# Edge attention on one core: the order of VectorE's steps in a round, and 186 column tiles in place of 169

## The chip, the cores and the metric

The kernel runs on one core of one Trainium2 chip. The metric is the device time of one execution in microseconds (us), the median of several runs. The core's engines work from queues of their own and wait for each other by semaphores: TensorE (PE, with its weight loads as PEld), VectorE (DVE), ScalarE (ACT), GpSimd (POOL) and SyncE (SP, which only issues DMAs here).

## The reference

A graph attention layer with a residual and a layer norm: 6250 nodes, 206250 edges sorted by destination, 128 features in 8 heads of 16.

```python
Qh = (h @ WQ).reshape(N, H, D); Kh = (h @ WK).reshape(N, H, D); Vh = (h @ WV).reshape(N, H, D)
Eh = (edge_attr @ WE).reshape(-1, H, D)
score = jnp.einsum('ehd,ehd,ehd->eh', Kh[src], Qh[dst], Eh) * inv_sqrt_d
score = jnp.exp(jnp.clip(score, -5.0, 5.0))
wV = segment_sum(Vh[src] * score[:, :, None], dst);  Z = segment_sum(score, dst)
return _layernorm(x + (wV / (Z[:, :, None] + 1e-06)).reshape(N, H * D))
```

## The kernel before

**Tiles and batches.** The edges lie in 1612 tiles of 128 edges, one edge in each partition. Four tiles make a batch; the last eight tiles make smaller ones, so that there are 406 batches. The main loop (L616) makes one round for each batch `b`, and the instructions of each engine run in the order in which the rounds write them: from batch 12 on the order is the one written by hand (L618).

**Where K and V of an edge come from.** Each edge needs the K and V rows of its source node. A table `kv` of both lies in HBM (L262). `gather` (L412) fetches the rows of one tile with one indirect DMA that GpSimd issues (L421), into the tile `kvrows` of the batch, two rounds ahead (`GLEAD`). From batch 18 on, a gather may start only when the batch `lag(b)` before it has had its Q rows expanded (L424, L350): the lag falls from 12 batches to 3 at batch 162, one batch in 16 rounds.

**Column tiles.** For 169 tiles there is no gather. The transposed node features lie in SBUF as `xz`: two f32 for each node, its feature and a zero. `columns` (L375) copies the column of each edge's source node into the tile `xcol`, and TensorE multiplies it with the K and V weights (L403); ScalarE then copies the product into `kvrows` (L410). ScalarE copies one column with one instruction (L394). VectorE copies two with one: it takes 8 bytes that begin with one node's feature and 8 bytes that end with the other's, and ors them (L390). The place of a column is known only on the chip: its offset is loaded into registers, one instruction for each group of columns (`addresses`, L363; the load is L369), and the loads of the next group stand in the queue ahead of the copies of this one (L381 to L394). A column tile is cut into 16 groups of 8: ScalarE copies ten, VectorE six (`COLV`). The first column tile is batch 26's, and then there is one in every 2.2 batches (`COLP`). `columns(b, v, most)` writes as many groups of engine `v` as are due at round `b`, at most `most`.

**A round on VectorE**, in the order of the queue: K times Q of batch b-1, from `kvrows` and the expanded Q in PSUM (L500); in even rounds the one-hots of two batches (`stage_0`, L461); one step of small work (`fill`, L608: a step of the bf16 split of Q rows, L297 to L300, or of a layer norm, L773 to L793); the product with the edge features (`kqe`, L503); in odd rounds the transposed one-hots of two batches (`stage_0t`, L477); a group of columns; a `fill`; the sum over each head (L506); a group of columns; the messages of batch b-2 (L548); what columns are still due; a `fill`; the clip of batch b-1 (L509); a `fill`. K times Q writes `kq`, which `kqe` reads; `kqe` writes what the head sum reads; the clip reads the head sum.

**The other engines in a round.** TensorE expands Q of batch b (L489, one PSUM bank, free when K times Q has read it), projects the edge features (L494, one bank, free when `kqe` has read it), now and then adds up windows of finished nodes (`finish`, L529), adds the messages of batch b-2 (L570), and projects a column tile (L403) and Q rows (L293). ScalarE copies finished windows (L541), raises the clipped scores of batch b-1 to their exponentials (`weigh`, L515 into the single PSUM tile `exp_p` and L517 into the message tile), copies the column tile's K and V (L410), copies its groups of columns (L394), and copies finished sums (L580). The layer norm of two blocks of nodes begins with L773, one round after the second of their `finish`.

Of the kernel before, what the change touches and what calls it, by code (L numbers as in the profile page):

```python
# [8 lines left out]
F32 = mybir.dt.float32  # L9
I32 = mybir.dt.int32  # L10
BF16 = mybir.dt.bfloat16
U8 = mybir.dt.uint8
# [4 lines left out]
P = 128  # L17
# [5 lines left out]
HW = 64  # L23
HALF = 16
DRIFT = 24
LEFT, RIGHT = 43, 128
XC = LEFT + N + RIGHT
MW = D + H
CH = 8
# [21 lines left out]
QLOOK = 3  # L51
QREG = 16
COL0 = 26
COLP = (11, 5)
COLN = 8
COLV = 6
COLL = 8
RING = 4096
SUMS = 8
XT_AT = RING + P  # L60
# [3 lines left out]
def cut_batches():  # L64
    out, t = [], 0
    while t < NT:
        k = B
        if t >= NT - TAIL:
            k = 2 if NT - t > 3 else 1
        out.append(range(t, t + k))  # L70
        t += k
    return out


def column_tiles():

    batches = cut_batches()
    at = (COL0 + k * COLP[0] // COLP[1] for k in range(len(batches)))
    return [batches[b][-1] for b in at if b < len(batches) and batches[b][-1] < NT - TAIL - 4 * B]
# [23 lines left out]
def edge_attention(ctx: ExitStack, tc: tile.TileContext, x, xT, srcT, srcC, dstT, dstB, dst0, bnd, lo, eaT,  # L103
                   wq, wkv, we, out, kv, qtab, qs, relD):
    nc = tc.nc
# [33 lines left out]
    with ExitStack() as fast:  # L139
# [102 lines left out]
        wp = fast.enter_context(tc.tile_pool(name="work", bufs=3))  # L242
# [61 lines left out]
        def build_q(until, now):  # L304

            while qwork or (now and len(built) < until):
                if not qwork:
                    qwork.append(q_rows(len(built)))
                if next(qwork[0], None) is None:
                    qwork.pop()  # L310
                if not now:
                    break
# [23 lines left out]
        def load_chunk(c):  # L336
            if c in chunks or c * CH >= NT:
                return
            n = min(CH, NT - c * CH) * P
            tl = ep.tile([P, CH * P], F32, name="ea")  # L340
            nc.sync.dma_start(tl[:, :n], eaT[:, c * CH * P:c * CH * P + n])
            chunks[c] = tl
# [11 lines left out]
        col_tiles, xz_bytes = {}, xz.rearrange("p n z -> p (n z)").bitcast(U8)  # L354
# [1 line left out]

        copied, projected = [0, 0], []

        runs = P // COLN
        kinds = [range(runs - COLV), range(runs - COLV, runs)]  # L360
        ahead = [None, None]

        def addresses(v):  # L363

            k, j = divmod(copied[v], len(kinds[v]))
            if k >= len(col_batches):
                return None
            j = kinds[v][j] * COLN
            return nc.values_load_multi_w_load_instructions(  # L369
                col_at[k % col_half:k % col_half + 1, k // col_half, j:j + COLN],  # L370
                engines=((mybir.EngineType.Activation, mybir.EngineType.DVE)[v],),
                min_val=XT_AT + 8 * LEFT - 4, max_val=XT_AT + 8 * (LEFT + N - 1),
                skip_runtime_bounds_check_because="edges name nodes")[1]

        def columns(b, v, most=runs):  # L375

            mine = kinds[v]
            due = int((b - COL0 + COLL) * len(mine) * COLP[1] / COLP[0] + 1e-6)
            while most and copied[v] < min(due, len(col_batches) * len(mine)):
                k, j = divmod(copied[v], len(mine))  # L380
                at = ahead[v] or addresses(v)  # L381
                copied[v] += 1
                ahead[v] = addresses(v)
                most -= 1
                if k not in col_tiles:
                    col_tiles[k] = wp.tile([P, P], F32, name="xcol", bufs=5)
                to, j = col_tiles[k].bitcast(U8), mine[j] * COLN
                if v:
                    for c in range(0, COLN, 2):
                        nc.vector.tensor_tensor(to[:, 4 * (j + c):4 * (j + c) + 8], xz_bytes[:, ds(at[c] - XT_AT, 8)],  # L390
                                                xz_bytes[:, ds(at[c + 1] - XT_AT, 8)], op=ALU.bitwise_or)
                else:
                    for c in range(COLN):
                        nc.scalar.copy(to[:, 4 * (j + c):4 * (j + c) + 4], xz_bytes[:, ds(at[c] - XT_AT, 4)])  # L394

        def project_columns(b):

# [8 lines left out]
        def place_columns():  # L406

            while projected:
                g, pk = projected.pop()
                nc.scalar.copy(g[:, B - 1, :], pk)  # L410
# [135 lines left out]
        def messages(b):  # L546
            n, g, m = st8[b]
            nc.vector.tensor_tensor(  # L548
                m[:, :n, :D].rearrange("p b (h d) -> p b h d", h=H),
                g[:, :n, D:].rearrange("p b (h d) -> p b h d", h=H),  # L550
                exp_p[:, :n, :, None].to_broadcast([P, n, H, DH]), op=ALU.mult)
# [47 lines left out]
        build_q(q_built(QLOOK + 2), True)  # L599
        nc.sync.dma_start(col_at, srcC.rearrange("(h p) e -> p h e", h=2))  # L600
        nc.vector.tensor_scalar(col_at, col_at, 8, XT_AT + 8 * LEFT, op0=ALU.mult, op1=ALU.add)
        odd = col_at[:, :, (runs - COLV) * COLN:].rearrange("k h (c z) -> k h c z", z=2)[:, :, :, 1]
        nc.vector.tensor_scalar(odd, odd, 4, None, op0=ALU.subtract)
        load_rel(0)
        for j in range(QLOOK):
# [2 lines left out]
        def fill():  # L608

            if qwork:  # L610
                build_q(0, False)
            elif norms and next(norms[0], None) is None:
                norms.pop(0)

        held = []
        for b in range(nbat + 3):  # L616
            if b >= XB and not manual:
                manual.append(fast.enter_context(tc.manual_schedule()))  # L618
            held += [(b + SLAG, store) for store in stores]
            stores.clear()  # L620
            if held and (held[0][0] <= b or b >= nbat):
                held.pop(0)[1]()
            if b < nbat:
                load_chunk(batches[b][0] // CH + EB - 3)
                load_rel(batches[b][0] // RC + 1)
                load_q(batches[b][0] // WT + QLOOK)
                g = gathered.pop(b)
                if b == min(XB, nbat - 1):
                    late_loads()
                if b == min(XB + 8, nbat - 1):  # L630
                    relative(C0, NT)
                if b == 14:
                    from_window(1)
                if b == 0:
                    stage_0t(0)
                stage_a(b, g)
                if b + GLEAD < nbat and b + GLEAD not in gathered:
                    gathered[b + GLEAD] = gather(b + GLEAD)
            norms.extend(pending)
            pending.clear()  # L640
            for _ in range(len(ready) if b >= nbat - 2 else 1):
                if ready:
                    finish(ready.pop(0))
            steps = stage_b(b - 1) if 0 <= b - 1 < nbat else iter(())
            next(steps, None)
            if b < nbat:
                stage_0(b)
            fill()
            next(steps, None)
            if b + 1 < nbat:  # L650
                stage_0t(b + 1)
            if b < nbat:
                columns(b, 1, 1)
            fill()
            next(steps, None)
            if b < nbat:
                columns(b, 1, 1)
            if 0 <= b - 2 < nbat:
                messages(b - 2)
            if b < nbat:  # L660
                columns(b, 1)
            fill()
            next(steps, None)
            fill()
            if 0 <= b - 1 < nbat:
                weigh(b - 1)
            place_columns()
            if b < nbat:
                columns(b, 0)
            if 0 <= b - 2 < nbat:  # L670
                stage_c(b - 2)
            if b < nbat:
                project_columns(b + GLEAD)
                build_q(q_built(min(NJ - 1, batches[b][0] // WT + QLOOK + 2)), True)
                if not qwork and len(built) < q_built(
                        min(NJ - 1, batches[min(nbat - 1, b + 3)][0] // WT + QLOOK + 2)):
                    qwork.append(q_rows(len(built)))
                    next(qwork[0])
            if b == min(60, nbat):
                count_inside()  # L680
            if b == min(80, nbat + 1):
                inside = nc.values_load(cnt_i[0:1, 0:1], min_val=0, max_val=2 * EPAD,
                                        skip_runtime_bounds_check_because="two counts of EPAD edges")
# [159 lines left out]
```

## Time and profile before

| what | value |
|---|---|
| time, median of 3 runs | 1865.27 us (1862.6 to 1865.44) |
| time of the profiled execution | 1863.48 us |
| its span, first to last instruction | 1861.6 us |
| mean granted TensorE clock | 0.927 |
| DVE, ACT, POOL, PE busy | 92%, 85%, 74%, 71% of the span |
| gathers issued by POOL | 1395 from `kv`, 48 from `x` at the start |
| pairs of columns on DVE, columns on ACT | 4056, 13520 |

The page of the profile gives the busy time of each engine and the costliest groups of instructions: count, busy time (overlaps counted once), mean duration of one, and the idle time of the engine just before them with what ended it. The duration of an instruction on DVE or ACT overlaps with the start of the next, so that the step from one start to the next is shorter than the duration. Loads into registers are instructions of an engine's sequencer (DVEq, ACTq) and are not counted as busy. A releaser called "issue" means that the engine waited for nothing that the profile shows other than its own sequencer.

### The profile page before, as it was taken

The numbers are of one execution on the slowest core, as the hardware profiler recorded it, in microseconds if no ns is written. First come the engines' busy times: TensorE is split into PE (matmuls) and PEld (weight loads), VectorE is DVE, ScalarE is ACT, GpSimd is POOL, SyncE is SP. The second block draws the span as 40 slices with busy tenths as digits, with TensorE's granted clock in tenths as the row PEclk, the third lists the DMA queues.
The fourth block names the chain that finished last, engine by engine and source line by source line (L and its number), as shares of the span: only waits on it lengthen the run. The fifth ranks groups of instructions, "written<-read, shape, count | busy, mean of one in ns | idle before, by whom it ended". The sixth has DMA issues, their size and how long they took to land.

```text
span 1861.6 us, 49514 instructions
## 1 busy us (share of the span) xinstructions
PE 1324.9 (71%) x9388; PEld 1156.1 (62%) x9388; DVE 1710.0 (92%) x7312; ACT 1576.9 (85%) x14716; POOL 1379.2 (74%) x1450
## 2 busy tenths in 40 slices
PE   5877777677677767777767776776767676777775
PEld 4766666566566666666656665665656665666665
DVE  6579999999999999999999999999999999999986
ACT  3327999899999999999999999999989998999950
POOL 7777777767777777677777777777777777777774
PEclk8888998899999999899998899899999999999997
DMA  9767677667766776677677667767766676677652
GB/s 303 228 214 217 184 217 206 197 187 207 212 199 183 212 214 184 209 214 208 183 225 210 190 188 225 206 184 211 224 202 185 202 223 190 196 200 233 205 173 68
DMA packets 170093, 377.79 MB, mean 203 GB/s; under 512 B 58305, under 2 KB 84245, under 8 KB 169775
## 3 DMA queue, kind: packets, MB, share of 16 engines
q0 software_dynamic: 68480, 186.02, 34.7%
q1 hardware_dynamic: 100155, 187.47, 33.6%
q14 instruction: 241, 1.97, 0.3%
q8 instruction: 77, 1.26, 0.3%
q10 hardware_dynamic: 1140, 1.06, 0.2%
HBM read 359.61 MB, written 14.81 MB: 201 GB/s over the span
## 4 chain that ended last, share of the span: by engine, by line
DVE 38%; DMA 17%; ACT 16%; PE 9%; POOL 7%; issue 6%; DVEq 5%; ACTq 2%; SPq 0%; POOLq 0%
DMA kvrows<-kv,src 14%; ACT xcol L394 13%; DVE xcol L390 7%; POOL kvrows L421 7%; DVE kqe L503 6%; DVE kq L500 6%; DVE sc L506 6%; DVE msg L548 5%; DVEq L369 5%; PE agg L570 3%; DVE onehotT L477 2%; PE eps L494 2%; ACTq L369 2%; PE finps L529 1%; DVE sc L509 1%
## 5 line engine op out<-in xcount | busy, mean ns | idle before, releaser
L421 POOL DMA_INDIRECT kvrows<-kv,src x1395 | 1329.7, 953 | 445.1 <-issue 307.7
L394 ACT COPY xcol<-xz 128x4 uint8 x13520 | 1364.8, 190 | 55.0 <-issue 49.4
L570 PE MATMUL agg<-msg,onehot 128*128 128x136 f32 x3224 | 511.6, 305 | 283.7 <-DVE msg L548 216.6
L570 PEld LDWEIGHTS agg<-msg,onehot 128*128 128x128 f32 x3224 | 442.0, 206 | 335.9 <-issue 302.6
L494 PE MATMUL eps<-we_sb,ea 128*128 128x128 f32 x3224 | 494.3, 299 | 149.3 <-DVE kqe L503 110.8
L494 PEld LDWEIGHTS eps<-we_sb,ea 128*128 128x128 f32 x3224 | 423.7, 205 | 200.2 <-DVE kqe L503 149.8
L390 DVE TENSOR_TENSOR xcol<-xz 128x8 uint8 x4056 | 399.5, 157 | 2.8 <-issue 1.7
L500 DVE TENSOR_TENSOR kq<-kvrows,qps 128x512 f32<-128x512 f32 x406 | 273.4, 673 | 38.3 <-DMA kvrows<-kv,src 29.0
L503 DVE TENSOR_TENSOR kqe<-kq,eps 128x512 f32<-128x512 f32 x406 | 274.5, 676 | 19.7 <-PE eps L494 4.7
L548 DVE TENSOR_TENSOR msg<-kvrows,exp_p 128x512 f32<-128x512 f32 x406 | 272.9, 672 | 4.6 <-ACT exp_p L515 4.6
L506 DVE TENSOR_REDUCE sc<-kqe 128x32 f32<-128x512 f32 x406 | 271.0, 667 | 0.5
L489 PE MATMUL qps<-qw,onehotT 126*128 126x128 bf16 x1612 | 168.6, 230 | 39.0 <-DVE kq L500 32.6
L489 PEld LDWEIGHTS <-onehotT 126*128 126x128 bf16 x1612 | 134.3, 103 | 84.9 <-issue 58.4
L515 ACT ACTIVATE exp_p<-sc 128x32 f32<-128x32 f32 x406 | 79.3, 195 | 92.1 <-DVE sc L509 79.3
L461 DVE TENSOR_TENSOR onehot<-iota_p,dst_sb 128x512 f32<-128x512 f32 x200 | 135.9, 680 | 3.0 <-PE agg L570 3.0
L529 PE MATMUL finps<-sum,shift 128*128 128x136 f32 x640 | 94.8, 292 | 30.0 <-ACT sum L580 29.8
L403 PE MATMUL colkv<-wkv_sb,xcol 128*128 128x256 f32 x338 | 114.5, 424 | 0.0
L477 DVE TENSOR_SCALAR onehotT<-relb,node 126x1024 bf16<-126x1024 bf16 (+2 forms) x206 | 103.7, 504 | 9.7 <-DMA relb<-relD 9.7
L529 PEld LDWEIGHTS finps<-sum,shift 128*128 128x128 f32 x640 | 83.3, 197 | 37.4 <-ACT sum L580 37.3
L517 ACT ACTIVATE msg<-sc 128x32 f32<-128x32 f32 x406 | 87.1, 215 | 0.1
L509 DVE TENSOR_SCALAR sc<-sc 128x32 f32<-128x32 f32 x406 | 77.0, 190 | 0.3
L421 POOL DMA_INDIRECT kvrows<-x,src x48 | 48.6, 1012 | 16.5 <-issue 12.2
(76 smaller groups left out, 567.2 us busy)
## 6 DMA issues: line engine op xcount, KB each, us to landing
ea<-eaT SPq DMA_DIRECT2D x201, 512.0 KB
relb<-relD SPq DMA_DIRECT2D x100, 504.0 KB
kvrows<-kv,src POOLq DMA_INDIRECT x1395
qw<-qs SPq DMA_DIRECT2D x202, 31.5 KB
kv<-ea SPq DMA_DIRECT2D x12, 512.0 KB
qs<-qst SPq DMA_DIRECT2D x48, 96.0 KB
xb<-x SPq DMA_DIRECT2D x24, 128.0 KB
out<-h SPq DMA_DIRECT2D x24, 128.0 KB
```

Source lines behind the costliest of these rows:

```text
L390: nc.vector.tensor_tensor(to[:, 4 * (j + c):4 * (j + c) + 8], xz_bytes[:, ds(at[c] - XT_AT, 8)], xz_bytes[:, ds(at[c + 1] - XT_AT, 8)], op ...
L394: nc.scalar.copy(to[:, 4 * (j + c):4 * (j + c) + 4], xz_bytes[:, ds(at[c] - XT_AT, 4)])
L421: ins = nc.gpsimd.indirect_dma_start(out=g[:k, i, :f], out_offset=None, in_=rows, in_offset=bass.IndirectOffsetOnAxis(ap=src_col(t)[:k], a ...
L477: nc.vector.tensor_scalar(ohT[:, :w], rels[t0 // RC][:, e0:e0 + w], node[:QROWS], None, op0=ALU.is_equal)
L489: expanded[b] = nc.tensor.matmul(pq[:, i, :], ohT[:, i * P:i * P + P], loaded[t0 // WT], start=True, stop=True)
L494: nc.tensor.matmul(pe[:, i, :], ea[:, i * P:i * P + P], we_sb, start=True, stop=True)
L500: nc.vector.tensor_tensor(t0[:, :n], g[:, :n, :D], pq[:, :n], op=ALU.mult)
L503: nc.vector.tensor_tensor(t1[:, :n], t0[:, :n], pe[:, :n], op=ALU.mult)
L506: nc.vector.tensor_reduce(sc[:, :n], t1[:, :n].rearrange("p b (h d) -> p b h d", h=H), axis=AX.X, op=ALU.add)
L529: nc.tensor.matmul(ps, shift[:, P - s:2 * P - s], sums[k // 2][:, k % 2], start=first and i == 0, stop=stop and i == len(parts) - 1)
L548: nc.vector.tensor_tensor(m[:, :n, :D].rearrange("p b (h d) -> p b h d", h=H), g[:, :n, D:].rearrange("p b (h d) -> p b h d", h=H), exp_p[ ...
L570: nc.tensor.matmul(aggs[u][:, 0 if final else k % 2], oh[:, i, :], m[:, i, :], start=not final and t % (2 * G) == 0, stop=tail)
```

## The change

The order of a round on VectorE becomes: K times Q of b-1; the one-hots (even rounds) or a `fill` and a group of columns (odd rounds); `kqe`; the transposed one-hots (odd) or a group of columns (even); two `fill`; the head sum; all columns that are still due; a `fill`; the clip of b-1; the messages of b-2, last in the round.

A column tile stands in every second batch from batch 26 on, which makes 186 of them (17 gathers fewer). A column tile has 50 columns on VectorE, in five groups of 10, and 78 on ScalarE, in nine groups of 8 or 9. So VectorE copies 186 x 25 = 4650 pairs, and ScalarE 186 x 78 = 14508 columns. With 2.5 groups due in a round, an odd round writes two groups and an even round three, one of them at the early place. The margins of `xz` shrink from 171 columns to 2, and `xcol` has six buffers in place of five.

```diff
-LEFT, RIGHT = 43, 128
+LEFT, RIGHT = 1, 1
...
-COLP = (11, 5)
-COLN = 8
-COLV = 6
+COLP = (2, 1)
+COLN = 9
+COL2 = 10
+COLV = 50
...
-        runs = P // COLN
-        kinds = [range(runs - COLV), range(runs - COLV, runs)]
+        mid = P - COLV
+        few, pairs2 = -(-mid // COLN), COLV // COL2
+        cut = [mid * i // few for i in range(few + 1)] + [mid + COL2 * (i + 1) for i in range(pairs2)]
+        pieces = list(zip(cut, cut[1:]))
+        kinds = [pieces[:few], pieces[few:]]
...
-            j = kinds[v][j] * COLN
+            i, j = kinds[v][j]
             return nc.values_load_multi_w_load_instructions(
-                col_at[k % col_half:k % col_half + 1, k // col_half, j:j + COLN],
+                col_at[k % col_half:k % col_half + 1, k // col_half, i:j],
...
-                    col_tiles[k] = wp.tile([P, P], F32, name="xcol", bufs=5)
+                    col_tiles[k] = wp.tile([P, P], F32, name="xcol", bufs=6)
...
-                    for c in range(0, COLN, 2):
+                    for c in range(0, e - i, 2):
...
             if b < nbat:
                 stage_0(b)
-            fill()
+            if b % 2:
+                fill()
+            if b < nbat and b % 2:
+                columns(b, 1, 1)
             next(steps, None)
             if b + 1 < nbat:
                 stage_0t(b + 1)
-            if b < nbat:
+            if b < nbat and b % 2 == 0:
                 columns(b, 1, 1)
             fill()
+            fill()
             next(steps, None)
-            if b < nbat:
-                columns(b, 1, 1)
-            if 0 <= b - 2 < nbat:
-                messages(b - 2)
             if b < nbat:
                 columns(b, 1)
             fill()
             next(steps, None)
-            fill()
+            if 0 <= b - 2 < nbat:
+                messages(b - 2)
             if 0 <= b - 1 < nbat:
                 weigh(b - 1)
```

More of the change, by code (lines that the diff above doesn't have):

```diff
@@ L373, in addresses, with columns @@
                 skip_runtime_bounds_check_because="edges name nodes")[1]
-        def columns(b, v, most=runs):
+        def columns(b, v, most=P):
             mine = kinds[v]
@@ L385, in columns @@
                 if k not in col_tiles:
-                    col_tiles[k] = wp.tile([P, P], F32, name="xcol", bufs=5)
-                to, j = col_tiles[k].bitcast(U8), mine[j] * COLN
+                    col_tiles[k] = wp.tile([P, P], F32, name="xcol", bufs=6)
+                to, (i, e) = col_tiles[k].bitcast(U8), mine[j]
                 if v:
-                    for c in range(0, COLN, 2):
-                        nc.vector.tensor_tensor(to[:, 4 * (j + c):4 * (j + c) + 8], xz_bytes[:, ds(at[c] - XT_AT, 8)],
+                    for c in range(0, e - i, 2):
+                        nc.vector.tensor_tensor(to[:, 4 * (i + c):4 * (i + c) + 8], xz_bytes[:, ds(at[c] - XT_AT, 8)],
                                                 xz_bytes[:, ds(at[c + 1] - XT_AT, 8)], op=ALU.bitwise_or)
                 else:
-                    for c in range(COLN):
-                        nc.scalar.copy(to[:, 4 * (j + c):4 * (j + c) + 4], xz_bytes[:, ds(at[c] - XT_AT, 4)])
+                    for c in range(e - i):
+                        nc.scalar.copy(to[:, 4 * (i + c):4 * (i + c) + 4], xz_bytes[:, ds(at[c] - XT_AT, 4)])
         def project_columns(b):
@@ L601, in edge_attention @@
         nc.vector.tensor_scalar(col_at, col_at, 8, XT_AT + 8 * LEFT, op0=ALU.mult, op1=ALU.add)
-        odd = col_at[:, :, (runs - COLV) * COLN:].rearrange("k h (c z) -> k h c z", z=2)[:, :, :, 1]
+        odd = col_at[:, :, mid:].rearrange("k h (c z) -> k h c z", z=2)[:, :, :, 1]
         nc.vector.tensor_scalar(odd, odd, 4, None, op0=ALU.subtract)
```

## The prediction

> **What bounds the kernel now.** I read first the busy times and the costliest groups on the page, then a count of rounds and of gathers in two stretches.
>
> ```profile
> PE 1324.9 (71%) x9388; PEld 1156.1 (62%) x9388; DVE 1710.0 (92%) x7312; ACT 1576.9 (85%) x14716; POOL 1379.2 (74%) x1450
> L421 POOL DMA_INDIRECT kvrows<-kv,src x1395 | 1329.7, 953 | 445.1 <-issue 307.7
> L394 ACT COPY xcol<-xz 128x4 uint8 x13520 | 1364.8, 190 | 55.0 <-issue 49.4
> ```
>
> DVE looks like the bound. But POOL's 74% hide something: its gathers have 307.7 us of idle time in front of them that nothing releases. The timeline of POOL shows the pattern:
>
> ```profile
> 1000.04 0.95 POOL L421 DMA_INDIRECT kvrows<-kv,src  x1 [0.30 <-issue]
> 1001.29 0.95 POOL L421 DMA_INDIRECT kvrows<-kv,src  x1 [0.30 <-issue]
> ```
>
> A gather takes 0.95 us and 0.30 us pass before the next, so POOL can't issue more than one in 1.25 us. The views by windows for K times Q (L500, one in a round), for the gathers (L421), and for all engines (PE, PEld, DVE, ACT, POOL), in this order:
>
> ```profile
> 420.00:780.00 360.00, 56.12 (x83) 0.95 0.68 201
> 800.00:1800.00 1000.00, 152.46 (x225) 0.94 0.70 204
> ```
> ```profile
> 420.00:780.00 360.00, 262.48 (x277) 0.95 0.68 201
> 800.00:1800.00 1000.00, 757.42 (x796) 0.94 0.70 204
> ```
> ```profile
> 420.00:780.00 360.00, 255.36 (x1877) 223.59 (x1878) 347.26 (x1555) 340.28 (x3261) 262.48 (x277) 0.95 0.68 201
> 800.00:1800.00 1000.00, 710.58 (x5124) 621.51 (x5123) 943.04 (x4192) 923.67 (x8784) 757.42 (x796) 0.94 0.70 204
> ```
>
> In the early stretch a round takes 360/83 = 4.34 us, and 277 gathers x 1.25 = 346 us leave POOL 14 us of slack. In the late one a round takes 1000/225 = 4.44 us, and 796 x 1.25 = 995 of 1000 us: POOL never rests. The waits of DVE in both stretches agree (early first):
>
> ```profile
> DVE rz L773 <- ACT fin L541: 4.6, 5, 1.4
> DVE qst L297 <- PE qrows L293: 3.7, 8, 0.7
> DVE kq L500 <- DMA kvrows<-kv,src: 0.3, 1, 0.3
> ```
> ```profile
> DVE kq L500 <- DMA kvrows<-kv,src: 18.7, 16, 3.0
> DVE rz L773 <- ACT fin L541: 15.4, 12, 2.3
> DVE qst L297 <- PE qrows L293: 9.7, 14, 2.1
> ```
>
> So there are two stages. Early, while the gathers still have a lead that shrinks, **DVE sets the round at 4.34**. Late, **POOL sets it at 4.44** and DVE waits for rows; without these 18.7 us (0.08 in a round) it would be near 4.36, so I take 4.34 as DVE's need throughout. Columns run over some 372 rounds (186 tiles in every second one); 4.34 fits about 147 times between the first load of offsets (144 us, below) and 780; 225 are late.
>
> **The change, part by part.** *Gathers.* 17 fall away: POOL's need falls to 3.5 x 1.25 = 4.375 in a round. If nothing else bound, 17 x 1.25 = 21 us would go, to 1842.
>
> *More pairs.* The rows of one round, and the offset loads:
>
> ```profile
> 1007.28 0.67 DVE L500 TENSOR_TENSOR kq<-kvrows,qps 128x512 f32<-128x512 f32 x1
> 1008.06 0.69 DVE L503 TENSOR_TENSOR kqe<-kq,eps 128x512 f32<-128x512 f32 x1
> 1008.67 0.48 DVE L477 TENSOR_SCALAR onehotT<-relb,node 126x1024 bf16<-126x1024 bf16 x1
> 1009.06 0.39 DVE L390 TENSOR_TENSOR xcol<-xz 128x8 uint8 x4
> 1009.37 0.68 DVE L506 TENSOR_REDUCE sc<-kqe 128x32 f32<-128x512 f32 x1
> 1009.97 0.38 DVE L390 TENSOR_TENSOR xcol<-xz 128x8 uint8 x4
> 1010.27 0.68 DVE L548 TENSOR_TENSOR msg<-kvrows,exp_p 128x512 f32<-128x512 f32 x1
> 1010.87 0.39 DVE L390 TENSOR_TENSOR xcol<-xz 128x8 uint8 x4
> ...
> 1012.06 0.69 DVE L500 TENSOR_TENSOR kq<-kvrows,qps 128x512 f32<-128x512 f32 x1 [0.71 <-issue]
> 1012.66 0.68 DVE L461 TENSOR_TENSOR onehot<-iota_p,dst_sb 128x512 f32<-128x512 f32 x1
> ```
> ```profile
> L369 ACTq TENSOR_LOAD <-col_at x1690: 537/557/1039, 148.0 to 1792.1; - x188
> L369 DVEq TENSOR_LOAD <-col_at x1014: 591/607/1211, 144.2 to 1787.7; - x169
> ```
> ```profile
> L390 DVE TENSOR_TENSOR xcol<-xz 128x8 uint8 x4056 | 399.5, 157 | 2.8 <-issue 1.7
> ```
>
> Four pairs end after 0.385 us, one lasts 0.157, so a further pair costs (0.385 - 0.157)/3 = 0.076. 4650 - 4056 = 594 pairs x 0.076 = **+45 us** of DVE.
>
> *The two products.* In the odd round above `kqe` begins 0.78 after K times Q, which it must await; in the even round the one-hots begin 0.60 after it. So an odd round whose `fill` is empty loses 0.18, of which (1008.06 - 1007.95) 0.11 is idle.
>
> ```profile
> L503 DVE TENSOR_TENSOR kqe<-kq,eps 128x512 f32<-128x512 f32 x84 | 57.1, 680 | 3.0
> DVE qst L297 <- PE qrows L293: 16.2, 26, 2.1
> ```
>
> The first row is the group of `kqe` in the early stretch: 3.0/0.11 = 27 of 84 rounds lost it, a third; 0.32 x 372 x 0.18 = **-22 us**, since a group of columns now stands between. What hides it if the offsets are late: nothing, and the 0.18 returns.
>
> *The Q rows.* The second row is the wait of the Q split over the whole run. It falls between the one-hots and `kqe`, in even rounds; there `fill` moves behind `kqe` and a group, about 1 us later. The waits average 0.6, so I count all of them off, with 0.08 of lost overlap each: 16.2 + 2.1 = **-18 us**. The wait of `rz` stays in its odd round, between the products. Steps of `fill` fall from 4 to 3.5 in a round; by the code 49 splits of 4 and 24 norms of 22 steps in 406 rounds need 1.8.
>
> *Messages and clip.* They cost the same at the new place. `exp_p` may now be written only after the messages of b-2 have read it, so ScalarE's exponential waits for the messages in place of the clip; both end the round on DVE. Behind it on ACT stand the column tile's copy and the round's columns. In return the messages that need it come nearly a round later, so ACT may lag further. TensorE starts its sums (L570) some 0.5 us later against `kqe`; it had room:
>
> ```profile
> 1011.10 1.16 PE L570 MATMUL agg<-msg,onehot 128*128 128x136 f32 x8 [1.13 <-DVE msg L548]
> 1013.99 1.16 PE L494 MATMUL eps<-we_sb,ea 128*128 128x128 f32 x8 [0.81 <-DVE kqe L503]
> ```
>
> 1.13 + 0.81 us idle in that round. I cost it at nothing; without that room PE would delay the next `kqe`. No DMA of SP changes its place.
>
> *The offset loads* are the open term. Now each group stands behind an instruction of 0.48 to 0.68 us that hides its load (L390's idle by issue: 1.7 us in all). After the change an even round has **two groups back to back** behind the head sum, and the second has only 0.385 us of copies to hide a longer load. A one-value load is in the trace too:
>
> ```profile
> L682 DVEq TENSOR_LOAD <-cnt_i x1: 309/309/309, 423.1 to 423.1; - x1
> L682 ACTq TENSOR_LOAD <-cnt_i x1: 282/282/282, 427.7 to 427.7; - x1
> 906.75 4.00 ACT L394 COPY xcol<-xz 128x4 uint8 x40
> ```
>
> From 309 to 607 ns for eight values is 43 ns a value, so 10 take 0.69 us (estimate). The sequencer must also hand each instruction to the engine, at a price h. On ACT 40 copies take (4.00 - 0.19)/39 = 0.098 each, 0.78 a group of 8; a load is 0.557 of it: h = 0.03. On DVE groups begin 0.91 and 0.90 apart (1009.06, 1009.97, 1010.87) with no idle time, so 0.607 + 5h is at most 0.905: h is at most 0.06. In an even round `kqe` is handed over 0.78 after the start of K times Q. From there the sequencer needs three loads and 12 hand-overs until the third group, 2.08 + 12h; the engine needs the rest of the one-hots (1.20 - 0.78 = 0.42), `kqe` 0.60, a group 0.385, the head sum 0.60 and a group 0.385: 2.39. The third group waits 0.05 (h = 0.03) to 0.41 us (h = 0.06). Steps of `fill`, in about half the rounds, take off some 0.05 on average. With h = 0.05, nearer the DVE row, I take 0.25: 186 x 0.25 = **+46 us**; the ends give 0 and +67.
>
> [...]
>
> *Sum.* 45 - 22 - 18 + 46 = +51 us over 372 rounds, +0.137 in a round: DVE's need becomes 4.477. Early: 147 x 0.137 = +20. Late: 4.477 - 4.444 = 0.033 x 225 = +7. The start and the tail stay. 1863.5 (the profiled execution, 1.8 under the median, within the spread of the runs) + 27 = **1891 us**.
>
> **Rivals.** *The loads stay hidden, and POOL's pace is what counts (faster).* If h on DVE is ACT's 0.03, the term is about nothing: 45 - 22 - 18 = +5, need 4.353, below POOL's 4.375. Early +2, late (4.375 - 4.444) x 225 = -15: **1850**. It decides where 147d + 225(4.34 + d - 4.444) is nothing, d = 0.063 in a round, or 0.10 us for each pair of groups. For it: L390 has no idle time by issue now. Against it: ACT, where groups do stand back to back, has 49.4 us of such idle time. [...]
>
> *ACT becomes the bound (slower still).* Its stretch from 200 to 1800 us, by lines:
>
> ```profile
> L394 ACT COPY xcol<-xz 128x4 uint8 x13120 | 1324.6, 190 | 51.4 <-issue 46.1
> L515 ACT ACTIVATE exp_p<-sc 128x32 f32<-128x32 f32 x363 | 70.7, 195 | 31.3 <-DVE sc L509 22.8 <-DVE mv L782 5.3 <-DVE w L789 0.6
> L541 ACT COPY fin<-finps 128x136 f32<-128x136 f32 x44 | 12.0, 273 | 34.1 <-PE finps L529 34.1
> ```
>
> Only the 31.3 us are slack for certain: (1600 - 31)/363 = 4.32 in a round. 988 more copies x 0.098 add 0.26: 4.58, less what groups of 9 hide (up to 51/363 = 0.14) and a later ACT no longer waits for finished windows (0.09). All gone, 4.35 and no bound; with half of the latter gone, 4.53: early 0.19 x 147 = 28, late 0.09 x 225 = 20: **1911**.
>
> *It balances.* With 0.1 us for a pair of groups the late gain pays for the early loss: **1863**.
>
> **How the numbers follow.** Forecast 0.46, ACT 0.10, POOL's pace 0.32, balance 0.12. A run can tell about 0.2% (4 us) from no change, so faster 0.32, same 0.12, slower 0.56. The upper end of the load term gives +72 us of DVE, 4.53 in a round and 1911 as well; the floor on the other side is 1842. The range reaches from 1845 to 1912. The forecast's own side is 1870 to 1912.
>
> **What would show it.** In the profile after: 1378 gathers from `kv`. L390's idle time by issue rises from 1.7 to about 46 us in all; if it stays below 18, the rival is right. The wait of L297 falls below 4 us, and `kqe`'s idle time in the early stretch from 3.0 to below 1. K times Q waits for rows less than 8 us in the late stretch (18.7 before), with DVE busy near 1755 us. Fewer than 83 rounds, about 80, lie between 420 and 780 us, and POOL is held by TensorE there. Had ACT become the bound, L515's waits would be near nothing and the messages would wait for it. What would make it wrong above all: a sequencer that runs further ahead than I give it, or an `rz` wait that changes with ACT's lag.

## The result and the profile after

The changed kernel takes **3213.64 us** (3203.01 to 3218.12), the kernel before 1864.31 us beside it: a ratio of 1.723, with a 95% interval of 1.719 to 1.728. The profiled execution took 3203.01 us, with a span of 3201.2 us and a mean granted clock of 0.727. The forecast of 1891 us and its range to 1912 us are both far below. In the main loop the lines of the kernel after have numbers 4 higher. In some of the sets of runs below the kernel before itself takes 2542 to 2580 us, so each time stands beside that of the kernel before in the same set.

The page of the kernel after, busy times and three groups:

```profile
PE 1711.3 (53%) x9422; PEld 1525.9 (48%) x9422; DVE 1821.0 (57%) x7906; ACT 1728.3 (54%) x15721; POOL 1357.8 (42%) x1433
...
L398 ACT COPY xcol<-xz 128x4 uint8 x14508 | 1514.9, 189 | 1258.5 <-issue 1237.4
L425 POOL DMA_INDIRECT kvrows<-kv,src x1378 | 1310.2, 951 | 1805.4 <-PE qps L493 1053.8
...
L394 DVE TENSOR_TENSOR xcol<-xz 128x8 uint8 x4650 | 446.7, 162 | 1031.0 <-issue 1010.6
```

No engine is the bound any more: the busiest stands still for 43% of the span. The idle time lies in front of the column copies of **both** engines, and its releaser is "issue": 1237.4 us on ACT (49.4 before) and 1010.6 us on DVE (1.7 before). The gathers wait for TensorE (1053.8 us), but no product waits for their rows: K times Q waits 0.2 us for them in the whole run (29.0 before). What the sequencers were doing is in the view of the loads (minimum, median, maximum in ns):

```profile
L373 ACTq TENSOR_LOAD <-col_at x1674: 550/1821/2667, 147.7 to 3138.2; - x186
L373 DVEq TENSOR_LOAD <-col_at x930: 1065/2287/2526, 139.3 to 3126.6; - x186
```

Before, eight values took 557 and 607 ns. Now eight or nine take 550 to over 2000 on ACT, and ten on DVE 1065 or about 2290. Rounds per stretch, by K times Q, and DVE's waits in the late stretch of the kernel after:

```profile
420.00:780.00 360.00, 29.95 (x44) 0.71 0.35 106
800.00:1800.00 1000.00, 84.51 (x125) 0.73 0.36 110
```
```profile
DVE xcol L394 <- issue: 335.3, 209, 2.4
DVE rz L778 <- ACT fin L545: 56.3, 8, 7.8
...
DVE kq L504 <- PE qps L493: 11.9, 7, 2.0
DVE qst L298 <- PE qrows L294: 1.9, 5, 0.4
```

A round takes 8.2 us early and 8.0 late, against 4.34 and 4.44: nearly the same loss in both stretches, all along. The timeline shows where it falls in an even round:

```profile
1003.86 0.68 DVE L510 TENSOR_REDUCE sc<-kqe 128x32 f32<-128x512 f32 x1
...
1006.24 0.47 DVE L394 TENSOR_TENSOR xcol<-xz 128x8 uint8 x5 [1.70 <-issue]
1006.54 0.95 ACT L398 COPY xcol<-xz 128x4 uint8 x9 [1.44 <-issue]
...
1008.64 0.95 ACT L398 COPY xcol<-xz 128x4 uint8 x9 [1.15 <-issue]
1008.86 0.47 DVE L394 TENSOR_TENSOR xcol<-xz 128x8 uint8 x5 [2.14 <-issue]
```

The place is the one that the forecast named: two groups behind the head sum. But both wait, 1.70 and 2.14 us where 0.25 was forecast for the second, and ScalarE, to which no wait was given, stands in the same way between its groups.

### The profile page after: what moved, and what is told of

Same layout as the page of the kernel before. It is cut to its first block, busy times and chain, and to the rows that moved or that the text cites. A ratio compares the mean times of both kernels' runs of the same rounds, so it can differ in the third digit from the quotient of the medians.

```text
span 3201.2 us, 50755 instructions
## 1 busy us (share of the span) xinstructions
PE 1711.3 (53%) x9422; PEld 1525.9 (48%) x9422; DVE 1821.0 (57%) x7906; ACT 1728.3 (54%) x15721; POOL 1357.8 (42%) x1433
## 3 DMA queue, kind: packets, MB, share of 16 engines
q1 hardware_dynamic: 100169, 187.39, 18.7%
q10 hardware_dynamic: 1140, 1.06, 0.1%
## 4 chain that ended last, share of the span: by engine, by line
issue 39%; ACT 37%; DVE 5%; ACTq 4%; PE 3%; POOL 3%; DMA 2%; DVEq 2%; POOLq 0%
ACT xcol L398 33%; ACTq L373 4%; POOL kvrows L425 3%; DMA kvrows<-kv,src 2%; DVEq L373 2%; PE finps L533 2%; ACT msg L521 1%; DVE xcol L394 1%; ACT kvrows L414 1%; PE agg L574 1%; ACT exp_p L519 1%; DVE kq L504 1%; ACT sum L584 1%; DVE msg L552 1%; DVE kqe L507 1%
## 5 line engine op out<-in xcount | busy, mean ns | idle before, releaser
L398 ACT COPY xcol<-xz 128x4 uint8 x14508 | 1514.9, 189 | 1258.5 <-issue 1237.4
L425 POOL DMA_INDIRECT kvrows<-kv,src x1378 | 1310.2, 951 | 1805.4 <-PE qps L493 1053.8
L574 PE MATMUL agg<-msg,onehot 128*128 128x136 f32 x3224 | 697.9, 381 | 1015.2 <-DVE msg L552 1004.7
L574 PEld LDWEIGHTS agg<-msg,onehot 128*128 128x128 f32 x3224 | 609.4, 273 | 1075.9 <-issue 912.3
L394 DVE TENSOR_TENSOR xcol<-xz 128x8 uint8 x4650 | 446.7, 162 | 1031.0 <-issue 1010.6
L498 PE MATMUL eps<-we_sb,ea 128*128 128x128 f32 x3224 | 599.3, 344 | 37.5 <-DVE kqe L507 34.9
L498 PEld LDWEIGHTS eps<-we_sb,ea 128*128 128x128 f32 x3224 | 536.7, 251 | 62.4 <-DVE kqe L507 56.3
L493 PE MATMUL qps<-qw,onehotT 126*128 126x128 bf16 x1612 | 212.3, 271 | 8.8 <-DVE kq L504 8.8
L493 PEld LDWEIGHTS <-onehotT 126*128 126x128 bf16 x1612 | 172.3, 128 | 84.4 <-issue 58.0
L407 PE MATMUL colkv<-wkv_sb,xcol 128*128 128x256 f32 x372 | 194.9, 627 | 0.0
L407 PEld LDWEIGHTS colkv<-wkv_sb,xcol 128*128 128x128 f32 x372 | 104.4, 335 | 0.0
```

The costliest lines, as they stand in the source:

```text
L394: nc.vector.tensor_tensor(to[:, 4 * (i + c):4 * (i + c) + 8], xz_bytes[:, ds(at[c] - XT_AT, 8)], xz_bytes[:, ds(at[c + 1] - XT_AT, 8)], op ...
L398: nc.scalar.copy(to[:, 4 * (i + c):4 * (i + c) + 4], xz_bytes[:, ds(at[c] - XT_AT, 4)])
L407: nc.tensor.matmul(pk, col_tiles.pop(k), wkv_sb, start=True, stop=True)
L425: ins = nc.gpsimd.indirect_dma_start(out=g[:k, i, :f], out_offset=None, in_=rows, in_offset=bass.IndirectOffsetOnAxis(ap=src_col(t)[:k], a ...
L493: expanded[b] = nc.tensor.matmul(pq[:, i, :], ohT[:, i * P:i * P + P], loaded[t0 // WT], start=True, stop=True)
L498: nc.tensor.matmul(pe[:, i, :], ea[:, i * P:i * P + P], we_sb, start=True, stop=True)
```

## The experiments

Three theories of the slow loads: **A (place)**, a load is fast only where its first value lies at a multiple of four values (16 bytes) in the table of offsets; **B (count)**, 9 and 10 values are slow wherever they lie; **C (order)**, loads are slow when they follow each other closely. For the rest of the loss: the order of VectorE's steps, or the 17 further tiles.

**e1: the kernel before, its table of offsets moved by one value.** Nothing else is changed, so all groups keep eight values.

```diff
-    col_at = cp.tile([col_half, 2, P], I32, name="col_at")
+    col_at = cp.tile([col_half, 2, P + 4], I32, name="col_at")[:, :, 1:P + 1]
```

> The kernel before with one edit: the table of offsets lies one value (4 bytes) further on, so that each group of eight starts off a boundary of four values; order of the round, counts and tiles are as before. Theory A (place): a load moves four values at a time only where the group starts at a multiple of four values, and the rest one by one at about 0.23 us each. Then all loads become slow, about 1.8 us on ACT and 1.85 on DVE, a tile takes ACT 10 x (1.82 + 0.24) = 20.6 us, and the time is 3600 to 3900 us. Rival B (count): loads are slow because they fetch more than eight values; then nothing changes here, 0.56 and 0.61 us, 1864 us. Rival C (order): the new order of the round makes the time; then 1864 us too.

3935.84 us (one run) beside 2550.34. Its loads:

```profile
L369 ACTq TENSOR_LOAD <-col_at x1690: 1732/1781/2544, 211.9 to 3866.6; - x188
L369 DVEq TENSOR_LOAD <-col_at x1014: 1837/1894/2269, 204.5 to 3848.8; - x169
```

All of them are slow, in the old order and with eight values each. B and C fall as the causes of slow loads; four bytes of address are enough.

**e4: the loads alone.** A kernel of register loads and copies that use them, each form eight times, with `i` and `j` as below.

```python
at = load(col[0:1, i:j], engines=(ACT,), min_val=0, max_val=8, skip_runtime_bounds_check_because="constants")[1]
use_act(at)
```

> No attention at all (the output is left zero): only loads into registers on ACT and then on DVE, eight times over, of 1 to 16 values at starts 0 to 4, each followed by copies that use the values. A (place): 8 values at start 0 and 4 take 0.56 us, at starts 1, 2 and 3 about 1.8; 1 value 0.28; 4 values at start 0 under 0.4, at start 1 near 0.95; 9 at start 0 0.80, 10 1.05, 12 0.83, 16 1.1; 9 at start 1 and 10 at start 2 above 2. B (count): up to 8 values all below 0.6 whatever the start, 9 and more near 2.

On ACT (L44 to L70; values `i:j` = 0:8, 1:9, 4:12, 0:4, 1:5, 0:9, 1:10) and on DVE (L105 and L109; 0:10, 2:12):

```profile
L44 ACTq TENSOR_LOAD <-col x8: 546/548/742, 1.0 to 264.1; - x8
L46 ACTq TENSOR_LOAD <-col x8: 1752/1762/6212, 8.2 to 265.4; - x8
L52 ACTq TENSOR_LOAD <-col x8: 545/550/1348, 29.7 to 273.3; - x8
L60 ACTq TENSOR_LOAD <-col x8: 311/312/318, 33.4 to 276.2; - x8
L62 ACTq TENSOR_LOAD <-col x8: 908/914/920, 34.1 to 276.9; - x8
L66 ACTq TENSOR_LOAD <-col x8: 786/786/792, 36.8 to 279.6; - x8
L70 ACTq TENSOR_LOAD <-col x8: 1965/1970/1977, 40.4 to 283.4; - x8
L105 DVEq TENSOR_LOAD <-col x8: 1059/1062/1062, 41.2 to 329.4; - x8
L109 DVEq TENSOR_LOAD <-col x8: 2293/2294/2301, 46.7 to 335.3; - x8
```

From a multiple of four, four values take 0.312 us and eight 0.548: about 0.24 for each four and 0.07 besides, and a rest of one or two costs 0.24 to 0.44 more (nine 0.786, ten 0.989). From one value further on four take 0.914, eight 1.762 and nine 1.970: 0.21 for **each value**. Starts at 2 and 3 gave the same for eight (1.756, 1.753). With these durations the offsets of one column tile can be added up. ScalarE's groups start at values 0, 8, 17, 26, 34, 43, 52, 60 and 69; five of the nine starts (17, 26, 34, 43, 69) are no multiple of four, and one of those five groups has eight values. So 2 x 0.548 + 2 x 0.786 + 4 x 1.970 + 1.76 = 12.3 us in two rounds, where the ten groups of eight took 5.5. VectorE's start at 78, 88, 98, 108 and 118, three of them off: 2 x 1.062 + 3 x 2.294 = 9.0, where six took 3.6 (6 x 0.607). Two rounds took 16.4 us. By the forecast's estimate of 0.03 us for handing over a copy (from 40 copies in 4.00 us on ACT; no run shows it by itself), 78 copies bring ACT's sequencer to 14.6 of them, the exponentials and other copies not counted: it had hardly any room left.

**e8 (e2 on another chip): the kernel after, each group at a multiple of twelve values in a padded table,** sizes kept.

```diff
-                col_at[k % col_half:k % col_half + 1, k // col_half, i:j],
+                col_pad[k % col_half:k % col_half + 1, k // col_half, 12 * g:12 * g + j - i],
```

(g is the number of the group; the table is filled once, ahead of the loop.)

> The kernel after with one edit: the groups keep their sizes (8 and 9, 10), but each starts at a multiple of 12 values in a padded table. A (place): loads fall to 0.56 (8 values), 0.80 (9) on ACT and 1.09 (10) on DVE; time 1950 to 2200 us, since the third group of an even round still waits more than 1 us. B (count): loads of 9 and 10 stay near 2 us and the time stays above 2900 us. C (order): 3200 us whatever the loads do.

> The kernel after with each group at a multiple of 12 values and its sizes (8 and 9, 10) kept, on another chip than the first time. A (place): loads of 0.56 and 0.80 us on ACT, 1.09 on DVE as in the first set; the third group of an even round waits about 1.3 us, so more than the 2011 us of the same order and tiles in eights, but far under 3213: 2050 to 2200 us.

e2: 2645.95 beside 2550.34, ratio 1.037 [1.030, 1.044]. e8: 2224.51 beside 1864.64, ratio 1.193 [1.191, 1.195], a little above what was expected. The load and the group of e8:

```profile
L373 DVEq TENSOR_LOAD <-col_pad x930: 1058/1089/1427, 142.1 to 2154.1; - x186
```
```profile
L394 DVE TENSOR_TENSOR xcol<-xz 128x8 uint8 x4650 | 447.4, 160 | 329.9 <-issue 308.2 <-DVE sc L510 0.5
```

The boundary alone gives 989 us back. But ten values from a good place still take 1.09 us, where the forecast had 0.69, and DVE still stands 308 us. The second of the two groups behind the head sum waits 0.88 us on average in this trace (all 600 waits of its groups: 0.51, the longest 1.4), where the forecast had 0.25.

**e7 (e3 on another chip): the kernel after in groups of eight,** with its order and its 186 tiles.

```diff
-COLN = 9
-COL2 = 10
-COLV = 50
+COLN = 8
+COL2 = 8
+COLV = 48
```

(VectorE's columns of a tile are then six groups in place of five, three in every round: two back to back in each of the 372 rounds, where the kernel after has them in every second one.)

> The kernel after, with its order and its 186 tiles, in groups of 8 (ten on ACT, six on DVE, so 48 columns on DVE in place of 50). A and B alike: loads of 0.56 and 0.61 us, 1850 to 1900 us. C (order): far above, near 3200 us. It also gives what order and tile count are worth once the loads are as before; the recorded forecast's terms with 48 columns and loads of 0.61 would put it near 1865 to 1880.

> Again the kernel after with its order and 186 tiles in groups of 8 (ten on ACT, six on DVE). On a chip where the kernel before takes 1864 us: A (place of the groups is all that went wrong) 1850 to 1890 us. C (the order or the tile count costs by itself): above 1930.

e3: 2635.73 beside 2550.34, 1.035 [1.028, 1.042]. e7: 2011.74 beside 1866.39, 1.079 [1.077, 1.081]. The expectation of e7 was missed: with the loads at 557 and 608 ns (medians) the change still costs 145 us. That is above the 1930 us which stood for C: the order or the further tiles cost by themselves. DVE stands 139.1 us by issue before its groups. The next three runs shared its chip: the kernel before once more, and one half of the change each.

> The kernel before, unchanged, for a trace beside the others. In the last set it took 2550 us where it had taken 1864, with the loads of the kernel in eights at their usual 0.56 and 0.61 us. Theory A: nothing in the kernel, the chip of that set kept the sequencers short of instructions; on another chip it is 1864 us again, and on the same one the trace shows idle time by issue in front of copies that follow no load. Rival: the time of this kernel swings by itself, and then the engines' waits for each other (rows, scores) carry the difference.

It took 1864.34 us, and its trace has 83 and 226 rounds in the two stretches.

**e5: the order alone,** which is e7 with 169 tiles.

```diff
-COLP = (2, 1)
+COLP = (11, 5)
```

> The order of the kernel after with 169 tiles in groups of 8, as before (ten on ACT, six on DVE). By the recorded terms the wait between the products and the wait of the Q split go, 40 us of DVE or 0.11 in a round; early -15 us, late nothing since POOL's 4.44 stays; two groups back to back cost up to 0.1 us in some rounds. Ratio 0.99 to 1.00. C: 1.03 or more.

1928.11, ratio 1.032 [1.031, 1.034]: missed. The wait of its column pairs over the whole run (us, times, longest), and its timeline of VectorE:

```profile
DVE xcol L394 <- issue: 103.7, 285, 1.0
```
```profile
600.90 0.68 DVE L507 TENSOR_TENSOR kqe<-kq,eps 128x512 f32<-128x512 f32 x1
601.50 0.48 DVE L481 TENSOR_SCALAR onehotT<-relb,node 126x1024 bf16<-126x1024 bf16 x1
601.89 0.68 DVE L510 TENSOR_REDUCE sc<-kqe 128x32 f32<-128x512 f32 x1
602.49 0.39 DVE L394 TENSOR_TENSOR xcol<-xz 128x8 uint8 x4
603.16 0.40 DVE L394 TENSOR_TENSOR xcol<-xz 128x8 uint8 x4 [0.29 <-issue]
```

The second of two groups begins 0.67 us behind the first: of the load between them (0.607) only what lies beside the first group's copies is hidden (0.385 us). The sequencer has no lead there, and the trace shows where it lost it. The head sum reads `kqe`, and the first load behind the head sum in the queue starts at 601.6, when `kqe` has just ended (600.90 + 0.68); the second starts at 602.5, with the first group's copies. From 300 to 1800 us this holds without exception: the 323 loads that stand right behind a head sum all start 0.05 us or more after the end of `kqe`, and the 162 that stand between `kqe` and the head sum all start before that end. In the kernel before it is the same (336 and 336), and in the kernel after too (186 and 93). So the sequencer stands at the head sum until `kqe` is done, and the loads of both groups behind it come after that.

**e6: the tiles alone,** 186 of them in the order of before, in eights (with the margins and the six buffers of the kernel after).

```diff
-COLP = (11, 5)
+COLP = (2, 1)
```

> The kernel before in its old order with a column tile in every second batch (186), groups of 8, the small margins and six column buffers. DVE has 12 pairs in a round in place of 10.9, +0.085 us, ACT 40 copies in place of 36.4, +0.36; POOL needs 4.375 in place of 4.44. Early slower (+12), late the same or slightly slower: ratio 1.00 to 1.02, with ACT as the engine that waits least.

1934.32, ratio 1.037 [1.035, 1.040]: missed too. What ACT still waits for in its early stretch, and DVE's longest wait there:

```profile
ACT fin L541 <- PE finps L529: 6.7, 10, 0.9
ACT xcol L394 <- issue: 5.7, 23, 0.5
```
```profile
DVE rz L773 <- ACT fin L541: 16.5, 5, 3.6
```

78 rounds lie there, 4.62 us each. These two are all of ACT's waits there, 12.4 of 360 us; it waits for no score, and the layer norm waits more than three times as long for ACT's copy as before (4.6). ACT is full; this is the ACT rival of the forecast, which gave 4.53.

**e9: e5 with no two groups back to back.** One group goes ahead of the clip, the rest behind the messages.

```diff
-                columns(b, 1)
+                columns(b, 1, 1)
             fill()
...
                 messages(b - 2)
+            if b < nbat:
+                columns(b, 1)
```

> The order of the kernel after with 169 tiles in eights (1928 us), and the columns still due behind the head sum split: one group there, the rest behind the messages. Theory D: what the order costs is the load of the second of two groups that stand back to back (about 104 us of DVE's idle time by issue there). Then this idle time falls below 20 us and the gains of the order remain, early rounds 0.1 us shorter: ratio 0.985 to 1.000, about 1850 us. Rival E: the late messages cost, since sums on TensorE begin behind them; then it stays near 1.03.

1868.27 beside 1864.64, ratio 1.0017 [1.0006, 1.0027], over 12 runs. Rounds by K times Q, and DVE's waits in the late stretch:

```profile
420.00:780.00 360.00, 56.03 (x83) 0.93 0.67 202
800.00:1800.00 1000.00, 152.20 (x225) 0.93 0.69 203
```
```profile
DVE kq L504 <- DMA kvrows<-kv,src: 20.6, 18, 3.5
DVE rz L780 <- ACT fin L545: 15.8, 14, 3.3
DVE xcol L394 <- issue: 9.9, 20, 0.9
```

So nearly all of the order's cost was the groups back to back (103.7 us of issue became 15.8, and 62 us of time became 4); rival E falls, since the messages are as late here. The gain that was expected beside it did not come: the rounds are those of before, 83 and 225. The late stretch is POOL's still, as its wait for rows (20.6; 18.7 before) shows. In the early one the waits that the change was to take off did go: the Q split's fell from 3.7 to 0.2 us, `kqe`'s from 3.0 to nothing. But the column groups now wait 3.0 by issue (0.3 before) and `rz` 5.9 (4.6), and DVE is busy 348.98 us (347.26 before) for as many rounds: hardly any time was freed.

**e10: the order of before, only a group or a fill between the products.**

```diff
-            fill()
+            if b % 2:
+                fill()
+            if b < nbat and b % 2:
+                columns(b, 1, 1)
             next(steps, None)
...
-            if b < nbat:
+            if b < nbat and b % 2 == 0:
                 columns(b, 1, 1)
             fill()
+            if b % 2 == 0:
+                fill()
```

> The kernel before with its messages and clip in their old places, and of the new order only the part between the products: a group of columns between them in odd rounds, no step of small work between them in even rounds. D: DVE loses 40 us of waits, early rounds 0.1 us shorter, late rounds stay with POOL: ratio 0.985 to 1.000. E: the same as D here, so that this and the run with the late messages differ only by what the place of the messages costs. A new wait would be the load in front of the early group of odd rounds, which stands right behind K times Q.

1875.17, ratio 1.0053 [1.0040, 1.0066]: missed, no gain from that place by itself; 16.7 us of issue came before the pairs.

**Larger groups on ScalarE, 186 or 169 tiles,** in the order of e9: e13 and e14 have 186 tiles in eights, e11, e15 and e17 186 with ScalarE's groups of 16, e12 and e16 169 with groups of 16. Against e9:

```diff
-COLP = (11, 5)
+COLP = (2, 1)
-COLN = 8
+COLN = 16
```

(The first pair alone in e13 and e14, the second alone in e12 and e16.) The question was whether 186 tiles cost time because ACT's sequencer is full (fewer, larger loads would give it back) or by the work of DVE and PE.

> The same with ACT's 80 columns of a tile in five groups of 16 (four fours in one load, 1.03 us by the loads measured alone, so (1.03 + 16 x 0.03)/16 = 0.094 a copy, under the engine's own 0.095). F: ACT gains 0.16 us a round, most of the cost of the tiles goes: ratio 1.00 to 1.015. G: no change against the run in eights, 1.03 to 1.04.

> 169 tiles, no two groups back to back, ACT's columns in sixteens. F: ACT gets room, but POOL still sets the late rounds at 4.44: ratio 0.985 to 1.000, ACT waiting longer for the messages. G: 1.000 to 1.003, as with eights.

> The order of the kernel after with no two groups back to back and 186 tiles in eights, ten groups on ACT and six on DVE. F and G alike: 1.03 to 1.04, as the tiles alone cost in the old order; DVE's idle time by issue below 30 us. If the back-to-back loads were also behind the tiles' cost, near 1.00.

> 186 tiles in eights in the new order, no two groups back to back, on a chip where the kernel before takes 1864 us. F and G alike: 1.03 to 1.04, with ACT's waits for the messages near nothing.

> The same with ACT's 80 columns of a tile in five groups of 16, 0.094 a copy by load and hand-over in place of 0.099. F: ACT gains 0.16 us a round and most of the cost of the tiles goes, 1.00 to 1.015. G: 1.03 to 1.04.

> 169 tiles in the new order, no two groups back to back, ACT's columns in sixteens, on a chip where the kernel before takes 1864 us. F: POOL still sets the late rounds: 0.985 to 1.000. G: 1.000 to 1.003.

> The order of e9 (no groups back to back), 186 tiles, ScalarE's groups of 16 in place of 8 (five loads a tile in place of ten), for a chip on which the kernel before takes about 1865 us. Theory F, ScalarE's sequencer is full (loads and copies together): five loads of 16 at about 1.03 us replace ten of 8 at 0.557, which saves 0.4 us a tile or 0.2 in a round, most of the 0.2 that e6 lost: ratio 1.00 to 1.02. Theory G, the tiles cost VectorE and TensorE their time and ScalarE's loads don't matter: 1.03 to 1.04 as in e6.

| run | us | before in its set | ratio, 95% interval |
|---|---|---|---|
| e13, 186 in eights | 2658.42 | 2580.38 | 1.029 [1.026, 1.032] |
| e11, 186 in sixteens | 2642.69 | 2580.38 | 1.025 [1.022, 1.028] |
| e12, 169 in sixteens | 2594.02 | 2580.38 | 1.006 [1.003, 1.008] |
| e14, 186 in eights | 2630.18 | 2548.07 | 1.033 [1.030, 1.036] |
| e15, 186 in sixteens | 2624.66 | 2548.07 | 1.030 [1.027, 1.032] |
| e16, 169 in sixteens | 2557.85 | 2548.07 | 1.0025 [0.9996, 1.0055] |
| e17, 186 in sixteens | 2615.60 | 2542.44 | 1.029 [1.023, 1.034] |

With 186 tiles the time is 2.5 to 3.3% longer with either size of group, and with 169 tiles groups of 16 gain nothing. All three sets ran where ACT waits 494 to 546 us by issue before its copies (last section), so they don't decide the question for a set in which the kernel before takes 1865 us. There e6's waits speak for ACT, and the kernel after narrows down what fills it: nine copies behind their load take 0.95 us there (timeline above), 0.095 from one to the next; in e6's early stretch the step is 0.099 with the loads between (0.098 over 40 copies in the kernel before). So of a round's 40 copies some 3.8 us are the copies themselves, and the loads add about 0.16 (estimate). That fewer loads would give so much back was not run there and stays **open**. No version beat the kernel before.

## Why the prediction was wrong

**The step that failed** is the sentence "From 309 to 607 ns for eight values is 43 ns a value, so 10 take 0.69 us (estimate)". It laid a line through one value and eight, both at good places, and took the length of a load to follow its count alone. Measured, ten values on VectorE took 1.06 us from a multiple of four and 2.29 from two values further on (e4); the median in the kernel after was 2.29. Before, every group started at a multiple of eight, so no row of its profile could show the difference; but the diff showed that the starts change: the new groups begin at 17, 78 and so on. The ends of the load term varied the hand-over price h between 0.03 and 0.06, while the duration of the load, the unmeasured number, had no bounds at all. That the kernel became slower, as forecast, is in part luck: 989 of the 1349 us come from the place of the loads, which stood in no term.

**The same step for ScalarE** was left out: the load term was worked out for VectorE only, and the ACT rival counted the groups of 9 as a gain, although five of ScalarE's nine loads a tile became more than three times as long (1.76 and 1.97 us by e4, where eight values took 0.557 before). In the kernel after they weigh more (12.3 against 9.0 us a tile, estimates from e4).

Where the 1349 us went, from sets in which the kernel before takes 1864 to 1866 us:

| step | us | difference |
|---|---|---|
| the kernel after | 3213.64 | |
| groups at good places (e8) | 2224.51 | -989 |
| groups of eight, so 48 columns of a tile on VectorE (e7) | 2011.74 | -213 |
| the kernel before, in e7's set | 1866.39 | -145 |

Of the last 145 us, 130 are found in the two halves: the order's groups back to back (e5: 1928.11 - 1866.39 = 62 us, gone in e9) and the further tiles (e6: 68 us).

Point by point. *Two stages, POOL at 1.25 us a gather late*: right for the kernel before, and e9 shows it again. *The gathers that fall away*: 1378, as said, of no use with longer rounds. *More pairs, +45 us*: the pairs' busy time rose from 399.5 to 446.7 us. *The two products and the Q rows, -22 and -18 us*: the waits did go (the Q split's 1.9 us in the late stretch, 9.7 before; `kqe`'s 0.1 us in the early one, 3.0 before), but e9 and e10 got no time for it. In e9's early stretch the waits for loads and of `rz` took back most of it; the lost overlap that the forecast counted as gain, 0.07 to 0.08 us each time, didn't show as less busy time. *Two groups back to back*: the place of the wait right, the size wrong twice, by the load (above) and by the sequencer's lead. The forecast let the sequencer run on from the hand-over of `kqe` through all three loads; in e5 it stands at the head sum until `kqe` has ended, and two of the loads come after that. With loads at the length of eight values the forecast's own sum of three loads gives 1.82 + 12 x 0.05 - 2.39 = 0.03 us, so that nearly nothing would wait. e5, with eight values, measured 103.7 us over 285 waits, 0.36 each. *Messages and clip at nothing*: in e9, with the messages behind the clip, ACT waits for them 26.7 us in the late stretch, and the time is that of before. *The ACT rival* had 0.10 of the chance; e6 gave its round within 0.1 us (4.62 against 4.53) for the tiles alone, in eights. *POOL's pace*, the rival with 1850, failed on the loads; e7, at 2012 us with all loads at good places, shows that it fails without that too.

## What to carry to other kernels

A load of several registers had a price by the address here and not only by the count (e4, ScalarE: eight values 0.548 us from a multiple of four, 1.762 from one value further on; from a multiple of four, ten 0.989 and twelve 0.797): keep each group's start and size at multiples of 16 bytes, and pad the table if the groups don't fit (e8: 989 us). When a change alters where something starts, look in the trace whether any row has such a start, and if none has, bound that duration itself, before the smaller terms. Of a load between two groups back to back only what lay beside the first group's copies was hidden here (e5: 0.607 us of load, 0.385 of copies, 0.29 of idle time); another instruction of 0.48 to 0.68 us between them hid one of eight values (1.7 us of idle time by issue in the whole kernel before). Count the sequencer's lead from the last instruction in the queue that has to wait for its input (here the head sum, which waits for `kqe`: 323 of 323 loads behind it in e5 start after `kqe`'s end).

## What the runs showed of the hardware

That a register load took 0.24 us for each four values from a multiple of four on, and 0.21 for each single value from one further on (e4), was not expected, nor that it is nearly the same on ScalarE and VectorE (eight values in e4: 0.548 and 0.595 us on their place, 1.762 and 1.856 off it).

The second finding is unexplained. In some sets the kernel before took 2542 to 2580 us, and the other kernels in these sets have loads of the usual length (e16: 0.607 us for eight values on VectorE, 1.034 for 16 on ScalarE). It isn't tied to the chip's number: the record gives the same one for the set of e8 to e10 (1864.64 us) and for that of e17 (2542.44), some 20 minutes later. ScalarE's timeline in e16 shows where:

```profile
1000.64 0.19 ACT L398 COPY xcol<-xz 128x4 uint8 x1 [0.44 <-issue]
1001.36 0.29 ACT L398 COPY xcol<-xz 128x4 uint8 x2 [0.52 <-issue]
1002.07 0.19 ACT L398 COPY xcol<-xz 128x4 uint8 x1 [0.43 <-issue]
1002.78 0.29 ACT L398 COPY xcol<-xz 128x4 uint8 x2 [0.52 <-issue]
...
1004.20 3.15 ACT L398 COPY xcol<-xz 128x4 uint8 x31 [0.50 <-issue]
```

In some stretches one or two copies come every 0.7 us, in others 31 run without a gap. These gaps add up to 534.3 us in e16 and to 48.8 us in the kernel before, run once more in e7's set. One view more, of ScalarE's loads from 999 to 1005 us:

```profile
L373 ACTq TENSOR_LOAD <-col_at x2: 1052/1053/1054, 1001.4 to 1004.6; - x2
```

Two loads lie there, each with its usual duration, and one of them (1001.4) before the gap ends at 1004.20; there are more gaps than loads, so the loads don't account for them. What does was not found.

The granted clock was 0.927 before, 0.876 in e7 and 0.727 after, where TensorE worked 1711.3 us for 9422 matmuls in place of 1324.9 for 9388. The lower clock can have cost little here (estimate): in the late stretch K times Q waited 11.9 us for TensorE in all, the Q split 1.9.
